# A gated two-way scan layer: its projections by Strassen's scheme with partial sums read from the banks, streamed by sixteen rows

## The chip, the core and the metric

The kernel runs on one NeuronCore of a Trainium2 chip, in float32. The metric is the device time of one execution in microseconds. The engines are PE (TensorE, matrix products), DVE (VectorE), ACT (ScalarE), POOL (GpSimd) and SP (SyncE, which issues all DMAs here); each runs its own queue in order, and they meet at semaphores. PE writes only to PSUM, eight banks of 128 partitions by 512 float32 values.

## What is computed

Four layers run one after another over four images of 512 channels by 64 by 64. Layer 0 is an attention layer, layer 1 a residual block of mixed-expert convolutions, layer 2 a linear attention. The change is in layer 3:

```python
C = input.shape[1]                                    # 512
x = jnp.einsum('bchw,oc->bohw', input, w_proj) + b_proj[None, :, None, None]
x_gate = x[:, :C]
x_scan = x[:, C:]
X_cum = _ds_cumsum(x_scan, discount, axis=2)          # y_t = d*y_{t-1} + x_t down the rows
X_cum = _ds_cumsum(X_cum, discount, axis=3)           # and along each row
gated = x_gate * jax.nn.sigmoid(X_cum)
return input + gamma * gated
```

The kernel runs the two sums in the other order, along the rows first, which gives the same.

So each image needs two products of a 512 by 512 weight with the 512 by 4096 image, one for the scan and one for the gate, two discounted running sums per channel, a sigmoid, a multiplication and the residual.

## The kernel before

An image lies in SBUF as four tiles `xs[pr]`, one per *pair* `pr` of column blocks: 128 partitions by four channel blocks (`kc`, or `m` for outputs) by 1024 columns, which are sixteen image rows. The images run one after another through `layer0` to `layer3`; while layer 3 of one image runs, tiles of the next are loaded as their buffers come free. PE's instructions keep the order in which the program writes them. The order on the other engines is set once, when the program is built: a planner takes, at its own reckoning of times, what is ready, earlier in the program first. Buffers come from pools with a fixed number each; where none is free, an instruction waits for the last reader of one. Two pools of PSUM matter: `pair_psum`, three tiles of two banks each, and `bank`, two tiles of one bank. Of SBUF pools, `bigp` has three tiles of 17 KB per partition, `xpool` five of 16 KB, `fourp` six of 4 KB, `blkp` seven of 2 KB, and `wlate` one of 16 KB.

Layer 2 ends with `add_values(pr, ms)` (lines 607 to 615, the products in L612, the addition in L615): for each channel block `m` two half-height products into a pair tile `wv`, which DVE adds to `xs`. Layer 3 then works by output channel block `m`. `scanned(m)` goes over the four pairs: eight products into a pair tile `ps` (L636), an ACT eviction with the bias into `s` (L638, tile `rows`), a DVE scan along the rows (L639), and an ACT copy that turns sixteen rows into columns of a second large tile `t` (L643, tile `cols`). When all 64 rows are there, four DVE scans run down the columns (L647), each followed by a sigmoid on ACT, written back in row order (L649). The scans take their discount from a tile `disc` whose entry at the start of each row or column is zero, so that one instruction of 1024 elements serves sixteen rows or columns. `gated(m, s)` makes eight products per pair into `pg` (L659), and DVE multiplies them with the sigmoids (L661) and adds the residual (L662); SP stores the result. The order is scanned 0, scanned 1, gated 0, scanned 2, gated 1, scanned 3, gated 2, gated 3; the additions of layer 2's values for pairs 1 to 3 stand between the products of scanned 0. The profile counts each float32 product of the program as two matmul instructions.

The weights `wproj` are loaded into `wlate` when layer 1's transformed values leave it (L76, issued after the last `conv2` in layer 2). `wc` (L358 to 361) is one `bigp` tile with layer 1's mixed weights and, behind them, `qs`, layer 2's query features.

Of the kernel before, what the change touches and what calls it, by code (L numbers as in the profile page):

```python
# [8 lines left out]
F32 = mybir.dt.float32  # L9
AF = mybir.ActivationFunctionType  # L10
ALU = mybir.AluOpType
# [3 lines left out]
B, C, H, W = 4, 512, 64, 64  # L15
P = 128
HW = H * W
NB = 512
NBLK = HW // NB
ROWS = NB // W  # L20
KC = C // P
D = 64
NT = HW // P
TPB = NB // P
NPAIR = NBLK // 2
E = 8
NPIECE = KC + 9 + KC
# [6 lines left out]
BQK, BPROJ, DISC, RB, SCALE, GAM2, GAM3 = 24, 25, 33, 37, 45, 46, 47  # L34
BQ2, BK2 = 48, 49
NPRM = 50
RING = 12


SUM_LO, SUM_HI = 1e-26, 1e30  # L40
# [3 lines left out]
def unshifted(ctx: ExitStack, tc: tile.TileContext, fits, x, wqkv_t, wout_t, router_t,  # L44
# [3 lines left out]
    nc = tc.nc  # L48
    const = ctx.enter_context(tc.tile_pool(name="const", bufs=1))
    wlate = ctx.enter_context(tc.tile_pool(name="wlate", bufs=1))  # L50
    xpool = ctx.enter_context(tc.tile_pool(name="xpool", bufs=5))
    bigp = ctx.enter_context(tc.tile_pool(name="bigp", bufs=3))
# [5 lines left out]
    def pair_psum(name):  # L58
        return ps.tile([P, 2, NB], F32, tag="s", name=name, bufs=3)

    def bank(name, shape=(P, NB)):
        return ps.tile(list(shape), F32, tag="acc", name=name)

    def four(name):
        return fourp.tile([P, 2, NB], F32, tag="four", name=name)

    def block(name, shape=(P, NB)):
        return blkp.tile(list(shape), F32, tag="blk", name=name)

    def flat(t):  # L70
        return t.rearrange("p h n -> p (h n)")

    def late_weights(src, shape, name):

        t = wlate.tile(shape, F32, tag="late", name=name)
        nc.sync.dma_start(t, src)  # L76
        return t

    def load_x(b):

        tiles = []
        for pr in range(NPAIR):
            t = xpool.tile([P, KC, 2 * NB], F32, tag="x", name=f"x_{b}_{pr}")
            nc.sync.dma_start(t, x[b, :, pr * 2 * NB:(pr + 1) * 2 * NB].rearrange("(kc p) n -> p kc n", p=P))
            tiles.append(t)
        return tiles


    wqkv_sb = const.tile([P, KC, 3 * D], F32, tag="wqkv", name="wqkv_sb")
    nc.sync.dma_start(wqkv_sb, wqkv_t.rearrange("(kc p) o -> p kc o", p=P))  # L90
    xs = load_x(0)
    prm_sb = const.tile([P, NPRM], F32, tag="prm", name="prm_sb")
    nc.sync.dma_start(prm_sb, prm)
    def col(i, n=1):
        return prm_sb[:, i:i + n]
# [17 lines left out]
    ones = const.tile([P, P], F32, tag="ones", name="ones")  # L113
# [241 lines left out]

    def layer1(b, xs, rw, mix):

        wcq = bigp.tile([P, NPIECE + 4 * NPAIR, P], F32, tag="big", name=f"wc_{b}")  # L358
        wc = wcq[:, 0:NPIECE, :]
        qs = wcq[:, NPIECE:, :].rearrange("p (a j) c -> p a (j c)", a=NPAIR)  # L360
        nc.scalar.copy(wc[:, 0:KC, :], mix)
        def mix_experts(j, n, pool, tag):
            ex = pool.tile([P, 4, E, P], F32, tag=tag, name=f"ex_{b}_{j}")
# [31 lines left out]
        for pr in range(NPAIR):  # L395
            y = pair_psum(f"c1_{b}_{pr}")
# [69 lines left out]
                nc.vector.scalar_tensor_tensor(xm, flat(y), bn_s[:, 2 + m:3 + m], xm, ALU.mult, ALU.add)  # L466
                nc.scalar.activation(xm, xm, AF.Relu, bias=bn_t[:, 2 + m:3 + m])

        return conv2, conv3, qs

    def layer2(b, xs, conv2, conv3, qs):

        ks = small.tile([P, NPAIR], F32, tag="ks", name=f"ks_{b}")
        g = bank(f"g_{b}", (P, C))
# [77 lines left out]
        h2[2] = conv2(2)  # L552
        conv3(1, h2[1])
        h2[3] = conv2(3)
        wproj_sb = late_weights(wproj_t.rearrange("(kc p) o -> p kc o", p=P), [P, KC, 2 * C], f"wproj_{b}")
        features(1, (0, 1))()
        conv3(2, h2[2])
        rest = features(0, (0, 1))
# [48 lines left out]
        def add_values(pr, ms=range(KC)):  # L607
            for m in ms:
# [4 lines left out]
                                     start=True, stop=True)  # L613
                xm = xs[pr][:, m, :]
                nc.vector.tensor_tensor(xm, flat(y), xm, ALU.add)  # L615
        return normed, add_values, wproj_sb

    def layer3(b, xs, normed, add_values, wproj_sb):


        def scanned(m):
            s = bigp.tile([P, HW], F32, tag="big", name=f"rows_{b}_{m}")
            t = bigp.tile([P, W, H], F32, tag="big", name=f"cols_{b}_{m}")
            disc = flat(four(f"disc_{b}_{m}"))
            nc.scalar.activation(disc, ones[:, 0:1].to_broadcast([P, 2 * NB]), AF.Copy, scale=col(DISC + m))
            nc.gpsimd.memset(disc.rearrange("p (r w) -> p r w", w=W)[:, :, 0:1], 0.0)
            for pr in range(NPAIR):
                if m == 0 and pr == 0:
                    add_values(0)
                blk = slice(pr * 2 * NB, (pr + 1) * 2 * NB)  # L630
                y = pair_psum(f"ps_{b}_{m}_{pr}")
                for h in range(2):
                    if m == 0 and pr + 1 < NPAIR:
                        add_values(pr + 1, (2 * h, 2 * h + 1))
                    for kc in range(KC):
                        nc.tensor.matmul(y[:, h, :], wproj_sb[:, kc, C + m * P:C + (m + 1) * P],  # L636
                                         xs[pr][:, kc, h * NB:(h + 1) * NB], start=kc == 0, stop=kc == KC - 1)
                nc.scalar.activation(s[:, blk], flat(y), AF.Identity, bias=col(BPROJ + KC + m))  # L638
                nc.vector.tensor_tensor_scan(s[:, blk], disc, s[:, blk], 0.0, ALU.mult, ALU.add)  # L639

                rows = s[:, blk].rearrange("p (h w) -> p w h", w=W)
                r0 = pr * 2 * ROWS
                nc.scalar.copy(t[:, :, r0:r0 + 2 * ROWS], rows)  # L643
            tf = t.rearrange("p w h -> p (w h)")
            for c in range(NPAIR):
                blk = slice(c * 2 * NB, (c + 1) * 2 * NB)
                nc.vector.tensor_tensor_scan(tf[:, blk], disc, tf[:, blk], 0.0, ALU.mult, ALU.add)  # L647
                c0 = c * 2 * ROWS
                nc.scalar.activation(s.rearrange("p (h w) -> p w h", w=W)[:, c0:c0 + 2 * ROWS, :],  # L649
                                     t[:, c0:c0 + 2 * ROWS, :], AF.Sigmoid)  # L650
            return s

        def gated(m, s):
            for pr in range(NPAIR):
                blk = slice(pr * 2 * NB, (pr + 1) * 2 * NB)
                y = pair_psum(f"pg_{b}_{m}_{pr}")
                for h in range(2):
                    for kc in range(KC):
                        nc.tensor.matmul(y[:, h, :], wproj_sb[:, kc, m * P:(m + 1) * P],  # L659
                                         xs[pr][:, kc, h * NB:(h + 1) * NB], start=kc == 0, stop=kc == KC - 1)  # L660
                nc.vector.scalar_tensor_tensor(s[:, blk], flat(y), col(BPROJ + m), s[:, blk], ALU.add, ALU.mult)  # L661
                nc.vector.scalar_tensor_tensor(s[:, blk], s[:, blk], col(GAM3), xs[pr][:, m, :],  # L662
                                               ALU.mult, ALU.add)
                nc.sync.dma_start(out[b, m * P:(m + 1) * P, blk], s[:, blk])

        sf = scanned(0)
        for m in range(KC):
            nxt = scanned(m + 1) if m + 1 < KC else None
            gated(m, sf)
            sf = nxt  # L670

    with tc.manual_schedule(engines={mybir.EngineType.PE}):
        for b in range(B):
            convs = layer1(b, xs, *layer0(b, xs))
            nxt = load_x(b + 1) if b + 1 < B else None
            tail = layer2(b, xs, *convs)
            layer3(b, xs, *tail)
            xs = nxt


    ends = small.tile([P, 2], F32, tag="ends", name="ends", bufs=1)
# [449 lines left out]
```

## Time and profile before

| | |
|---|---|
| median of the runs | 2866.96 us (2866.65 to 2868.54, three runs) |
| the profiled execution's own time | 2869.1 us |
| its span | 2867.2 us |
| PE busy in it | 2785.5 us, 97% |
| DVE busy | 1817.0 us, 63% |
| ACT busy | 1182.1 us, 41% |
| mean granted clock of PE | 0.991 |

The profile is of one execution; spans and times are in microseconds unless marked ns. Its groups of instructions give a line of the kernel, engine, operation, output and input by the program's names, shapes and count, then busy time, mean duration of one, and the idle time of the engine just ahead of them with what ended it. PEld are weight loads, which run beside products. Matmuls are pipelined, so the time from one start to the next is shorter than the duration of one. The chain that ended last is followed back from the last instruction to what released it each time.

### The profile page before, as it was taken

How to read it: one execution, taken by the hardware profiler on the slowest of the kernel's cores; microseconds unless marked ns; L12 is line 12 of the kernel's file. 1: busy time of each engine (PE TensorE's matmuls, PEld its weight loads, DVE VectorE, ACT ScalarE, POOL GpSimd, SP SyncE). 2: the span in 40 equal slices, each digit the busy share in tenths (PEclk: the TensorE clock that was granted, in tenths of full speed). 3: DMA queues.
4: the chain of work that ended last, by engine and by line, in shares of the span. 5: the costliest groups of instructions: out<-in, count | busy, mean ns of one | idle time of the engine just before them, and what ended most of it. 6: DMA issues, size and time to landing. Idle time of an engine off the chain costs nothing.

```text
span 2867.2 us, 24918 instructions
## 1 busy us (share of the span) xinstructions
PE 2785.5 (97%) x10174; PEld 1178.8 (41%) x10174; DVE 1817.0 (63%) x1827; ACT 1182.1 (41%) x1131; POOL 11.4 (0%) x34
## 2 busy tenths in 40 slices
PE   8999989999999999999999998999999999899998
PEld 3333444444333344444433334544443333454443
DVE  2687866564378786555437879566544786956644
ACT  4545243443454414353344442535334544143531
POOL 1000000000000000000000000000000000000000
PEclk9999999999999999999999999999999999999999
DMA  4000210011300021001220002100131000100001
GB/s 178 1 1 0 96 59 1 0 52 59 125 1 1 1 95 59 1 0 59 86 90 1 1 1 95 59 1 6 53 118 58 1 1 28 68 30 1 22 37 60
DMA packets 31485, 115.12 MB, mean 40 GB/s; under 512 B 2432, under 2 KB 3456, under 8 KB 31360
## 3 DMA queue, kind: packets, MB, share of 16 engines
q1 hardware_dynamic: 31360, 113.43, 10.4%
q8 instruction: 82, 1.34, 0.2%
q14 instruction: 43, 0.35, 0.0%
HBM read 79.86 MB, written 33.55 MB: 40 GB/s over the span
## 4 chain that ended last, share of the span: by engine, by line
PE 85%; DVE 11%; ACT 2%; issue 1%; DMA 0%; SPq 0%; ACTq 0%; DVEq 0%
PE s L213 16%; PE av L228 16%; PE ps L636 16%; PE pg L659 15%; PE z L485 4%; PE kq L174 4%; PE c L464 3%; DVE wc L368 2%; PE wv L612 2%; PE vv L174 2%; PE xtr L527 2%; PE g L544 2%; PE c L444 1%; PE y L267 1%; DVE nrm L573 1%; DVE t L412 1%
## 5 line engine op out<-in xcount | busy, mean ns | idle before, releaser
L213 PE MATMUL s<-qv,key 64*128 64x512 f32 x2048 | 468.8, 602 | 1.8 <-ACT ring L216 1.8
L636 PE MATMUL ps<-x,wproj 128*128 128x512 f32 x1024 | 447.2, 595 | 0.0
L221 DVE TENSOR_TENSOR acc<-acc,ring 128x1024 f32<-128x1024 f32 x312 | 381.7, 1224 | 100.0 <-ACT ring L216 71.3
L659 PE MATMUL pg<-x,wproj 128*128 128x512 f32 x1024 | 441.4, 592 | 0.0
L216 ACT ACTIVATE ring<-s 128x1024 f32<-128x1024 f32 x336 | 317.6, 1038 | 223.8 <-PE s L213 223.5
L639 DVE TENSOR_TENSOR_SCAN rows<-disc,rows 128x1024 f32<-128x1024 f32 x64 | 146.7, 2292 | 259.4 <-ACT rows L638 237.4
L228 PE MATMUL av<-ring,qv 128*64 128x512 f32 x1344 | 304.5, 595 | 0.0
L213 PEld LDWEIGHTS s<-qv,key 64*128 64x128 f32 x2048 | 189.0, 187 | 274.9 <-issue 172.9
L636 PEld LDWEIGHTS ps<-x,wproj 128*128 128x128 f32 x1024 | 192.8, 190 | 251.7 <-issue 242.3
L659 PEld LDWEIGHTS pg<-x,wproj 128*128 128x128 f32 x1024 | 194.7, 190 | 244.7 <-issue 242.8
L221 DVE TENSOR_TENSOR acc<-acc,ringx 128x1024 f32<-128x1024 f32 x168 | 205.5, 1223 | 102.4 <-ACT ringx L216 90.1
L216 ACT ACTIVATE ringx<-s 128x1024 f32<-128x1024 f32 x176 | 172.1, 1040 | 207.0 <-PE s L213 207.0
L638 ACT ACTIVATE rows<-ps,prm_sb 128x1024 f32<-128x1024 f32 x64 | 71.0, 1110 | 290.6 <-PE ps L636 290.6
L643 ACT COPY cols<-rows 128x1024 f32<-128x1024 f32 x64 | 125.6, 1963 | 151.9 <-DVE rows L639 151.9
L228 PEld LDWEIGHTS av<-ring,qv 128*64 128x64 f32 x1344 | 93.4, 137 | 198.5 <-issue 198.5
L228 PE MATMUL av<-ringx,qv 128*64 128x512 f32 x704 | 167.2, 598 | 0.0
L647 DVE TENSOR_TENSOR_SCAN cols<-disc,cols 128x1024 f32<-128x1024 f32 x64 | 141.4, 2272 | 32.4 <-ACT cols L643 32.4
L464 PE MATMUL c<-h,wc 128*128 128x512 f32 x256 | 125.3, 644 | 33.6 <-ACT h L456 33.6
L661 DVE SCALAR_TENSOR_TENSOR rows<-pg,prm_sb,rows 128x1024 f32<-128x1024 f32 x64 | 81.8, 1278 | 116.6 <-PE pg L659 116.6
L649 ACT ACTIVATE rows<-cols 128x1024 f32<-128x1024 f32 x64 | 128.1, 2002 | 41.3 <-DVE cols L647 41.3
L174 PE MATMUL kq<-x,wqkv_sb 128*64 128x512 f32 x512 | 115.8, 606 | 9.5 <-DMA x<-in_x_dram 9.0
L466 DVE SCALAR_TENSOR_TENSOR x<-c,bn_s,x 128x1024 f32<-128x1024 f32 x64 | 81.3, 1281 | 56.3 <-PE c L464 56.3
(162 smaller groups left out, 2529.5 us busy)
## 6 DMA issues: line engine op xcount, KB each, us to landing
x<-in_x_dram SPq DMA_DIRECT2D x16, 2048.0 KB, 8.6
out_dram<-rows SPq DMA_DIRECT2D x64, 512.0 KB, 2.6
ex<-in_experts_dram SPq DMA_DIRECT2D x12, 1536.0 KB, 9.5
ex<-in_experts_dram SPq DMA_DIRECT2D x8, 2048.0 KB, 9.5
wproj<-in_wproj_t_dram SPq DMA_DIRECT2D x4, 2048.0 KB, 10.1
wv_sb<-in_wv_t_dram SPq DMA_DIRECT2D x1, 1024.0 KB, 9.6
wqkv_sb<-in_wqkv_t_dram SPq DMA_DIRECT2D x1, 384.0 KB, 3.3
wout_sb<-in_wout_t_dram SPq DMA_DIRECT2D x2, 128.0 KB, 13.9
```

Of the source, the lines that this page charges most:

```text
L174: nc.tensor.matmul(y[h * D:(h + 1) * D, :], wqkv_sb[:, kc, col0:col0 + D], xs[pr][:, kc, h * NB:(h + 1) * NB], start=kc == 0, stop=kc == K ...
L213: nc.tensor.matmul(s[:, h, :], key[r, kt * P:(kt + 1) * P], qry[r, pr * NB:(pr + 1) * NB], start=True, stop=True)
L216: nc.scalar.activation(p, s, AF.Exp)
L221: nc.vector.tensor_tensor(accs[pr], accs[pr], p, ALU.add)
L228: nc.tensor.matmul(avs[pr][h * D:(h + 1) * D, :], vt[:, kt, :], ring[i % RING][:, h, :], start=kt == 0, stop=kt == NT - 1)
L464: nc.tensor.matmul(y[:, h, :], wc[:, KC + 9 + m, :], h2[:, h, :], start=True, stop=True)
L636: nc.tensor.matmul(y[:, h, :], wproj_sb[:, kc, C + m * P:C + (m + 1) * P], xs[pr][:, kc, h * NB:(h + 1) * NB], start=kc == 0, stop=kc == K ...
L639: nc.vector.tensor_tensor_scan(s[:, blk], disc, s[:, blk], 0.0, ALU.mult, ALU.add)
L643: nc.scalar.copy(t[:, :, r0:r0 + 2 * ROWS], rows)
L647: nc.vector.tensor_tensor_scan(tf[:, blk], disc, tf[:, blk], 0.0, ALU.mult, ALU.add)
L649: nc.scalar.activation(s.rearrange("p (h w) -> p w h", w=W)[:, c0:c0 + 2 * ROWS, :], t[:, c0:c0 + 2 * ROWS, :], AF.Sigmoid)
L659: nc.tensor.matmul(y[:, h, :], wproj_sb[:, kc, m * P:(m + 1) * P], xs[pr][:, kc, h * NB:(h + 1) * NB], start=kc == 0, stop=kc == KC - 1)
```

## The change

The product of weights and image is cut two by two: weights by output half and input half, the image by input half (channel blocks 0, 1 and 2, 3) and by the two blocks of 512 columns in a pair. Seven products of 256 by 256 by 512 take the place of eight, in Winograd's form of Strassen's scheme. A *tile* `(pr, j)` yields, for one pair, the output blocks `j` and `j + 2`; a `Sums` block makes it for the scan and a `Gates` block for the gate. An image has eight tiles. Iteration `i` of a loop of nine runs the Sums of tile `i` and the Gates of tile `i - 1`, product by product in turn; the first and the last iteration have one block alone.

Each block has one bank `x`, in which products 1, 6, 7 and 4 are added up one after another, and a pair `zy`, with product 2 in one bank and 5 and 3 in the other. After products 1, 6 and 7 ACT evicts the running sum of `x` with the bias into `e[0..2]`, each before the next product is added to that bank. DVE forms the four outputs from `zy`, `x` and `e`. The four sums of weights S1 to S4 are formed on DVE when the quarters of the weights have come, by eight loads in place of one; the sums of image parts T1 to T4 are formed per pair by four DVE subtractions and additions, after its values have been added.

The scans no longer wait for all 64 rows: each tile scans its sixteen rows along, turns them by ACT, adds the carried state of the row above (`carry`, times the discount) to the first entry of each column, scans down sixteen rows, keeps the last entry as the next carry, and takes the sigmoid. Scans are half as long (512), with one discount tile `along` for the rows and one `down`, reset when `j` changes, for the columns. `add_values` steps of the next pair stand ahead of product 2 of a block. The loads of the next image's tiles are issued inside the loop, every second iteration.

```diff
-        wcq = bigp.tile([P, NPIECE + 4 * NPAIR, P], F32, tag="big", name=f"wc_{b}")
+        wcq = bigp.tile([P, NPIECE + 1 + 4 * NPAIR, P], F32, tag="big", name=f"wc_{b}")
         wc = wcq[:, 0:NPIECE, :]
-        qs = wcq[:, NPIECE:, :].rearrange("p (a j) c -> p a (j c)", a=NPAIR)
+        qs = wcq[:, NPIECE + 1:, :].rearrange("p (a j) c -> p a (j c)", a=NPAIR)
         nc.scalar.copy(wc[:, 0:KC, :], mix)
...
-        wproj_sb = late_weights(wproj_t.rearrange("(kc p) o -> p kc o", p=P), [P, KC, 2 * C], f"wproj_{b}")
+        weights = load_quarters(b)
...
+    def load_quarters(b):
+        wq = wlate.tile([P, 4, 2, 2, 2 * P], F32, tag="late", name=f"wq_{b}")
+        sx = xpool.tile([P, 4, 2, 2, 2 * P], F32, tag="x", name=f"sx_{b}")
+        wr = wproj_t.rearrange("(k c p) (s m o) -> k c m p s o", c=2, p=P, s=2, m=2)
+        for q, (m, k) in enumerate(((0, 0), (0, 1), (1, 1), (1, 0))):
+            for c in range(2):
+                nc.sync.dma_start(wq[:, q, c], wr[k, c, m])
+        a11, a12, a22, a21 = (wq[:, q] for q in range(4))
+        s2, s3, s4 = (sx[:, q] for q in range(3))
+        fl = lambda t: t.rearrange("p c s o -> p (c s o)")
+        nc.vector.tensor_tensor(fl(s3), fl(a11), fl(a21), ALU.subtract)
+        nc.vector.tensor_tensor(fl(a21), fl(a21), fl(a22), ALU.add)
+        nc.vector.tensor_tensor(fl(s2), fl(a21), fl(a11), ALU.subtract)
+        nc.vector.tensor_tensor(fl(s4), fl(a12), fl(s2), ALU.subtract)
+        spare = fl(sx[:, 3]).rearrange("p (i n) -> p i n", i=2)
+        nc.gpsimd.memset(fl(sx[:, 3]).rearrange("p (w r) -> p w r", r=R2)[:, :, 0], 0.0)
+        return {1: a11, 2: a12, 3: s4, 4: a22, 5: a21, 6: s2, 7: s3}, spare
+    def layer3(b, xs, add_values, weights, wcq):
+        weights, down = weights
+        carry = wcq[:, KC * TPB:KC * TPB + 2, :].rearrange("p i (m w) -> p (i m) w", w=W)
+        others, rowsums, cols = {}, {}, {}
+        along = wcq[:, 0:KC * TPB, :].rearrange("p (m j) c -> p m (j c)", m=KC)
+        nc.gpsimd.memset(along.rearrange("p m (r w) -> p (m r) w", w=W)[:, :, 0], 0.0)
+        for m in range(KC):
+            nc.scalar.activation(along[:, m, :].rearrange("p (r w) -> p r w", w=W)[:, :, 1:],
+                                 ones[:, 0:1, None].to_broadcast([P, ROWS, W - 1]), AF.Copy, scale=col(DISC + m))
+        def set_down(j):
+            for i in range(2):
+                nc.scalar.activation(down[:, i, :].rearrange("p (w r) -> p w r", r=R2)[:, :, 1:],
+                                     ones[:, 0:1, None].to_broadcast([P, W // 2, R2 - 1]), AF.Copy,
+                                     scale=col(DISC + j + 2 * i))
+            cols["set"] = j
+        def sum_x(pr):
+            t = bigp.tile([P, 4, 2, NB], F32, tag="big", name=f"t_{b}_{pr}")
+            xv = xs[pr].rearrange("p k (h n) -> p k h n", h=2)
+            b11, b12, b21, b22 = xv[:, 0:2, 0], xv[:, 0:2, 1], xv[:, 2:4, 0], xv[:, 2:4, 1]
+            t1, t2, t3, t4 = (t[:, i] for i in range(4))
+            nc.vector.tensor_tensor(t3, b22, b12, ALU.subtract)
+            nc.vector.tensor_tensor(t2, t3, b11, ALU.add)
+            nc.vector.tensor_tensor(t1, b12, b11, ALU.subtract)
+            nc.vector.tensor_tensor(t4, b21, t2, ALU.subtract)
+            others[pr] = {1: b11, 2: b21, 3: b22, 4: t4, 5: t1, 6: t2, 7: t3}
+        class Block:
+            def __init__(self, kind, pr, j):
+                self.kind, self.pr, self.j = kind, pr, j
+                name = f"{b}_{kind}_{pr}_{j}"
+                self.name = name
+                self.x = bank(f"sx_{name}")
+                self.zy, self.done = None, set()
+                self.bias = [col(BPROJ + kind * KC + m) for m in (j, j + 2)]
+                self.e = [block(f"e{i}_{name}") for i in range(3)]
+            def product(self, k):
+                if k == 2:
+                    self.zy = pair_psum(f"zy_{self.name}")
+                y = self.x if k in (1, 6, 7, 4) else self.zy[:, 0 if k == 2 else 1, :]
+                w, v = weights[k], others[self.pr][k]
+                for c in range(2):
+                    nc.tensor.matmul(y, w[:, c, self.kind, self.j * P:(self.j + 1) * P], v[:, c, :],
+                                     start=c == 0 and k in (1, 2, 5), stop=c == 1,
+                                     skip_group_check=k not in (1, 2, 5))
+                self.done.add(k)
+                if k in (1, 6, 7):
+                    i = (1, 6, 7).index(k)
+                    nc.scalar.activation(self.e[i], y, AF.Identity, bias=self.bias[i // 2])
+                if k in (5, 7) and {5, 7} <= self.done:
+                    self.fifth()
+                elif k == 4:
+                    self.fourth()
+        class Sums(Block):
+            def fifth(self):
+                self.s = [flat(four(f"s{i}_{self.name}")) for i in range(2)]
+                nc.vector.tensor_tensor(self.s[1][:, NB:], self.zy[:, 1, :], self.e[2], ALU.add)
+            def fourth(self):
+                nc.scalar.activation(self.s[1][:, :NB], self.x, AF.Identity, bias=self.bias[1])
+            def end(self):
                 for h in range(2):
...
+                    nc.vector.tensor_tensor(self.s[0][:, h * NB:(h + 1) * NB], self.zy[:, h, :], self.e[h], ALU.add)
+                if cols.get("set") != self.j:
+                    set_down(self.j)
+                for i in (1, 0):
+                    m, s = self.j + 2 * i, self.s[i]
+                    for h in range(2):
+                        sh = s[:, h * NB:(h + 1) * NB]
+                        nc.vector.tensor_tensor_scan(sh, along[:, m, :], sh, 0.0, ALU.mult, ALU.add)
+                    sr = s.rearrange("p (r w) -> p w r", w=W)
+                    tf = flat(four(f"t{i}_{self.name}"))
+                    t = tf.rearrange("p (w r) -> p w r", w=W)
+                    nc.scalar.copy(t, sr)
+                    if self.pr > 0:
+                        nc.vector.scalar_tensor_tensor(t[:, :, 0], carry[:, m, :], col(DISC + m), t[:, :, 0],
+                                                       ALU.mult, ALU.add)
+                    for h in range(2):
+                        th = tf[:, h * NB:(h + 1) * NB]
+                        nc.vector.tensor_tensor_scan(th, down[:, i, :], th, 0.0, ALU.mult, ALU.add)
+                    if self.pr < NPAIR - 1:
+                        nc.scalar.copy(carry[:, m, :], t[:, :, R2 - 1])
+                    nc.scalar.activation(sr, t, AF.Sigmoid)
+                rowsums[self.pr, self.j] = self.s
+        class Gates(Block):
+            def fifth(self):
+                self.s = rowsums.pop((self.pr, self.j))
+                nc.vector.tensor_tensor(self.e[2], self.zy[:, 1, :], self.e[2], ALU.add)
+            def fourth(self):
+                s = self.s[1][:, :NB]
+                nc.vector.scalar_tensor_tensor(s, self.x, self.bias[1], s, ALU.add, ALU.mult)
+                s = self.s[1][:, NB:]
+                nc.vector.tensor_tensor(s, s, self.e[2], ALU.mult)
+                self.add_x(1)
+            def end(self):
                 for h in range(2):
...
+                    e, s = self.e[h], self.s[0][:, h * NB:(h + 1) * NB]
+                    nc.vector.tensor_tensor(e, self.zy[:, h, :], e, ALU.add)
+                    nc.vector.tensor_tensor(s, s, e, ALU.mult)
+                self.add_x(0)
+            def add_x(self, i):
+                m, s = self.j + 2 * i, self.s[i]
+                nc.vector.scalar_tensor_tensor(s, s, col(GAM3), xs[self.pr][:, m, :], ALU.mult, ALU.add)
+                nc.sync.dma_start(out[b, m * P:(m + 1) * P, self.pr * 2 * NB:(self.pr + 1) * 2 * NB], s)
+        tiles = [(pr, (pr + j) % 2) for pr in range(NPAIR) for j in range(2)]
+        between = {0: [(1, 0), (1, 1)], 1: [(1, 2), (1, 3)], 2: [(2, 0), (2, 1)], 3: [(2, 2), (2, 3)],
+                   4: [(3, 0), (3, 1)], 5: [(3, 2), (3, 3)]}
+        nxt = []
+        add_values(0)
+        sum_x(0)
+        for i in range(len(tiles) + 1):
+            blocks = [Sums(1, *tiles[i])] if i < len(tiles) else []
+            blocks += [Gates(0, *tiles[i - 1])] if i else []
+            todo = list(between.get(i, ()))
+            for n, k in enumerate((1, 2, 6, 7, 5, 4, 3) if len(blocks) > 1 else (1, 2, 6, 5, 7, 4, 3)):
+                for s in blocks:
+                    if n in (1, 3) and todo:
+                        pr, m = todo.pop(0)
+                        add_values(pr, (m,))
+                        if m == KC - 1:
+                            sum_x(pr)
+                    s.product(k)
+            for s in blocks:
+                s.end()
+            if i and i % 2 == 0 and b + 1 < B:
+                nxt.append(load_pair(b + 1, i // 2 - 1))
+        return nxt
...
             convs = layer1(b, xs, *layer0(b, xs))
-            nxt = load_x(b + 1) if b + 1 < B else None
-            tail = layer2(b, xs, *convs)
-            layer3(b, xs, *tail)
-            xs = nxt
+            xs = layer3(b, xs, *layer2(b, xs, *convs))
```

Of the lines with a minus sign the diff above leaves out the bodies of `scanned` and `gated`, which are told in the section on the kernel before.

More of the change, by code (lines that the diff above doesn't have):

```diff
@@ L37 @@
 RING = 12
+R2 = 2 * ROWS
 SUM_LO, SUM_HI = 1e-26, 1e30
@@ L77, in late_weights, with load_pair @@
         return t
[L79 to L86, printed above, removed]
+    def load_pair(b, pr):
+        t = xpool.tile([P, KC, 2 * NB], F32, tag="x", name=f"x_{b}_{pr}")
+        nc.sync.dma_start(t, x[b, :, pr * 2 * NB:(pr + 1) * 2 * NB].rearrange("(kc p) n -> p kc n", p=P))
+        return t
     wqkv_sb = const.tile([P, KC, 3 * D], F32, tag="wqkv", name="wqkv_sb")
     nc.sync.dma_start(wqkv_sb, wqkv_t.rearrange("(kc p) o -> p kc o", p=P))
-    xs = load_x(0)
+    xs = [load_pair(0, pr) for pr in range(NPAIR)]
     prm_sb = const.tile([P, NPRM], F32, tag="prm", name="prm_sb")
@@ L467, in conv3, with layer2 @@
                 nc.scalar.activation(xm, xm, AF.Relu, bias=bn_t[:, 2 + m:3 + m])
-        return conv2, conv3, qs
-    def layer2(b, xs, conv2, conv3, qs):
+        return conv2, conv3, wcq, qs
+    def layer2(b, xs, conv2, conv3, wcq, qs):
         ks = small.tile([P, NPAIR], F32, tag="ks", name=f"ks_{b}")
@@ L615, in add_values @@
                 nc.vector.tensor_tensor(xm, flat(y), xm, ALU.add)
[L616 to L631, printed above, removed]
-                for h in range(2):
[L633 to L656, printed above, removed]
-                for h in range(2):
[L658 to L670, printed above, removed]
@@ new lines, in layer2 @@
+        return add_values, weights, wcq
+    def load_quarters(b):
[15 more added lines that the diff above has]
+        return {1: a11, 2: a12, 3: s4, 4: a22, 5: a21, 6: s2, 7: s3}, spare
```

## The prediction, made before the change was run

> **What bounds the kernel now.** I read the page's busy shares first, then the chain that ended last, then the groups and the windows of layer 3, and last the order of time where layer 3 starts.
>
> ```profile
> PE 2785.5 (97%) x10174; PEld 1178.8 (41%) x10174; DVE 1817.0 (63%) x1827; ACT 1182.1 (41%) x1131; POOL 11.4 (0%) x34
> PE 85%; DVE 11%; ACT 2%; issue 1%; DMA 0%; SPq 0%; ACTq 0%; DVEq 0%
> PE s L213 16%; PE av L228 16%; PE ps L636 16%; PE pg L659 15%; PE z L485 4%; PE kq L174 4%; PE c L464 3%; DVE wc L368 2%; PE wv L612 2%; PE vv L174 2%; PE xtr L527 2%; PE g L544 2%; PE c L444 1%; PE y L267 1%; DVE nrm L573 1%; DVE t L412 1%
> ```
>
> PE is busy 97% of the span, and layer 3's two products (ps, pg) are 31% of the chain: fewer matmuls there shorten the end, as long as nothing takes PE's place.
>
> ```profile
> L636 PE MATMUL ps<-x,wproj 128*128 128x512 f32 x1024 | 447.2, 595 | 0.0
> L659 PE MATMUL pg<-x,wproj 128*128 128x512 f32 x1024 | 441.4, 592 | 0.0
> L639 DVE TENSOR_TENSOR_SCAN rows<-disc,rows 128x1024 f32<-128x1024 f32 x64 | 146.7, 2292 | 259.4 <-ACT rows L638 237.4 <-issue 22.0
> L647 DVE TENSOR_TENSOR_SCAN cols<-disc,cols 128x1024 f32<-128x1024 f32 x64 | 141.4, 2272 | 32.4 <-ACT cols L643 32.4
> L643 ACT COPY cols<-rows 128x1024 f32<-128x1024 f32 x64 | 125.6, 1963 | 151.9 <-DVE rows L639 151.9
> L649 ACT ACTIVATE rows<-cols 128x1024 f32<-128x1024 f32 x64 | 128.1, 2002 | 41.3 <-DVE cols L647 41.3
> L662 DVE SCALAR_TENSOR_TENSOR rows<-rows,prm_sb,x 128x1024 f32<-128x1024 f32 x64 | 82.3, 1285 | 2.3
> L615 DVE TENSOR_TENSOR x<-wv,x 128x1024 f32<-128x1024 f32 x64 | 74.4, 1216 | 22.3 <-PE wv L612 22.3
> L447 DVE TENSOR_TENSOR dq<-c,sp 128x512 f32<-128x512 f32 x16 | 11.0, 689 | 35.7 <-ACT sp L446 35.7
> L446 ACT COPY sp<-c 128x512 f32<-128x512 f32 x16 | 9.4, 585 | 70.7 <-PE c L444 70.7
> ```
>
> The columns are busy us, mean ns of one, idle before. The two matmul groups have no idle at all; those on DVE and ACT wait for PE or for each other.
>
> ```profile
> 1236.00:1438.60 202.60, 202.60 (x474) 89.52 (x475) 106.64 (x62) 79.44 (x51) 0.00 (x0) 1.00 0.16 60
> ```
>
> This is layer 3 of the second image: length, then busy PE, PEld, DVE, ACT. PE is full, DVE has 96 us to spare, ACT 123. Next come PE's chain and timeline rows.
>
> ```profile
> 1273.78 27.47 PE pg L659 x64
> ...
> 1080.76 9.73 PE L464 MATMUL c<-h,wc 128*128 128x512 f32 x16 [8.41 <-ACT h L456]
> ...
> 1098.10 7.03 PE L464 MATMUL c<-h,wc 128*128 128x512 f32 x16
> ...
> 1208.00 3.70 PE L636 MATMUL ps<-x,wproj 128*128 128x512 f32 x8
> 1211.63 1.99 PE L612 MATMUL wv<-wc,kv 64*128 64x512 f32 x8
> ```
>
> 64 matmuls in 27.47 us is 0.429 each, the price used below (the 592 ns is latency). Eight wv are 1.95 us, so one add_values step (four) is 0.98; 1211.63 − 1208.00 − 8 × 0.429 leaves 0.2 us for the switch to them.
>
> **Matmuls, on the path.** An image now issues 1024 / 4 × 2 = 512 (each counted product is two instructions). The change issues 8 tiles × 2 kinds × 7 products × 2 halves of the sum × 2 instructions = 448. 64 × 0.429 = 27.5 us an image, 109.9 in four. A product is 4 × 0.429 = 1.72 us, a full iteration (seven for Sums S, seven for Gates G) 24.0, with two add_values steps ("mixed", iterations 1 to 5) 26.0, plus 2 × 0.2.
>
> **DVE, beside it.** From 1.22 us for 1024 elements and 0.69 for 512 the fixed part is 0.16, so a half scan is (2.28 + 0.16) / 2 = 1.22; its bounds are 1.14 (half the row) and 2.29. A tile's Sums: 3 × 0.69 + 8 × 1.22 + two column fixes of 64 elements (between the 0.15 and 0.28 us of the smallest rows; 0.2, in six of eight tiles) = 12.1. Its Gates: 7 × 0.69 + 2 × 1.28 = 7.4. Together 19.5; a mixed iteration adds 2 × 1.22 for the value sums and, every other time, 4 × 1.22 for T1 to T4: 24.4 on average, against PE's 26.4. Over the image that is 196 of some 208 us, where 129 of 236 are used now (106.6 in the window above, 22 before it). DVE fits, with next to no slack, so order decides.
>
> **ACT** per tile: four copies and sigmoids 8.0, seven evictions 0.6 each, two carry copies and the discount rows about 1.2: 13.4 of 24. It fits too.
>
> **The new wait.** A mixed iteration wants four pair buffers (step, S's, step, G's) from three. G's product 2 needs the first step's buffer, so its addition on DVE. From PE's end of a tile (t = 0) unhindered PE wants that buffer at t = 7.1. DVE, taking early whatever is ready early: S's product 4 ends at −5.15, evicted by −4.3; first-half scan of the upper rows to −3.1; G's fourth step (0.69 + 0.69 + 1.28) to −0.4; S's last addition to 0.3; column scans with fix to 3.0; one row scan to 4.2; G's end (same three sizes) to 6.8. ACT meanwhile runs sigmoid 3.0 to 5.0, copy to 7.0. If the addition, ready at 4.6, goes next, it ends at 8.0 and PE waits 1.0 us; if the column scans behind the copy go first, 3.8. The trace cannot show this order, fixed at build; a step put early would wait 0. I take the middle of the two, 2.4, × 5 = 12.0 us an image. All of PE's later products queue behind G's product 2.
>
> **Small terms per image.** Three evictions per block must read the bank x between products that add to it. Nearest rows: ACT starts some 0.2 after PE, 0.59 for the read. Bare, 16 blocks × 3 × 0.8 = 38 us, more than the gain; but the other block's 1.72 us product lies between. What shows is the single-block iterations 0 and 8, where product 4 follows 7: 0.9 each, 1.8. In iterations 6 and 7 a read of G behind a 2.0 us sigmoid: 0.4 each, 0.8. Six more switches to wv than now: 1.2. Weight sums, 4 × 1.22 = 4.9 on DVE in layer 2: 0 if in the idle 11.8 us that DVE has near 1163, 4.9 if ahead of key transposes; 1.5. Sum with the wait: 17.3 us.
>
> The Trainium skill, "PSUM — Partial Sum Buffer", section on bank collisions, says that two engines must never touch one bank at once, even at other addresses; that speaks against reading running sums. By it alone, with no interleaving, the 38 us above would stand.
>
> **Edits at nothing.** The eight weight loads bring the same 2 MB as wproj (10.1 us to landing) in 1 KB runs; four times the first small-run load (384 KB in 3.3) gives 13.2. They are issued near 1113 and needed 90 us later; uncovered, 10 to 13 an image. The x loads go out tile by tile on SP behind the stores; the last is issued just as layer 0 starts and its pair is multiplied 32 us later (kq 1438.6 to 1470.9), against 8.6 to land. Discount rows: ACT and POOL, under 3 us, in ACT's idle time. T1 to T4 of pair 0 lie beside two products. The tail, one half-size step more: 1 us once.
>
> **Sum.** −109.9 + 4 × 17.3 + 1 = −39.7 us. The profiled execution has span 2867.2 and time 2869.1, so 2827.5 and 2829.4; applied to the median of 2866.96, which is 2.1 below the profiled time, 2827.
>
> **Rivals.**
> *Whole gain*: DVE's planned order puts the value additions early, so that PE never waits; 1.8 + 1.2 = 3.0 an image stay: −109.9 + 12 + 1 = −97, 2770. For it: DVE's 24.4 is below 26.4. Against it: its work comes in one run of 11 us at each tile's end, just when PE wants buffers.
> *Slower*: DVE's queue becomes the bound. Its place is the tile's end: each column scan waits at the queue's head for its 2.0 us copy, with ready additions behind it. A mixed iteration is then 24.4 + 2 × 2.0 = 28.4 against 26.4, so 2.0 + 3.8 = 5.8 × 5 = 29.0, with 1.8 + 0.8 + 1.2 + 4.9: 37.7 an image, −109.9 + 150.8 + 1 = +42, 2909. It decides from 27.2 us of waits an image, 4.4 per mixed iteration with the 5.3 of small terms. For it: L647's idle is all waits for that copy, once per four scans now, twice per tile then. Against it: other ready work is there to fill the 2 us.
> *Clock*: after the 8.41 us wait above, 16 matmuls took 9.73 instead of 7.03, 2.7 lost; after the 1.3 us wait ahead of the first wv (24 in 5.85) nothing. My waits lie nearer the second, so nothing is taken.
>
> The Trainium skill, "TensorE: Matmul & The Clock Gate", section on the HAM clock gate, halves the clock after an idle window of about 3.4 us; if each 3.8 us wait did that, up to 1.7 us estimated each, 34 us in all, would come on top. The rows here show only the 8.41 us case.
>
> That fewer matmuls are not issued is excluded by the loops.
>
> **How the numbers follow.** The forecast, 2800 (waits of 1.0) to 2870 (waits of 3.8, weight sums uncovered), has 0.47, of which 0.06 falls within 0.2% (5.7 us, about what a measurement can tell from no change). Whole gain: 0.23. Slower: 0.30, as DVE's slack is 2 us in 26 and I cannot see its order. Faster is 0.41 + 0.23 = 0.64, same 0.06, slower 0.30. The range, 2767 to 2900, takes in the whole gain and most of the slower case.
>
> **What would show it.** Right: about 1792 layer 3 matmuls at 0.429; DVE near 87% busy (195 of 225 us) between layer 3's start and end; layer 3 near 225 us an image instead of 236; PE waiting before products for value additions (x). Whole gain: PE without gaps there. Wrong: DVE full and PE's gaps of 4 us or more in each mixed iteration, or gaps on ACT's evictions, which I count at almost nothing; or layer 2 longer by over 5 us an image.

## The result, and the profile after

The changed kernel takes 3004.81 us (3002.67 to 3007.02) against 2867.19 for the kernel before: 1.0479 times as long (95% interval 1.0461 to 1.0497), 138 us more, beyond the range of 2767 to 2900. These are lines of the page of the changed kernel: the span, the busy time of each engine with its instructions, and the costliest groups in question (busy time and mean ns of one, then the idle time before them).

```profile
span 3003.7 us, 25338 instructions
...
PE 2760.3 (92%) x9918; PEld 1145.7 (38%) x9918; DVE 2044.3 (68%) x2339; ACT 1277.6 (43%) x1379; POOL 10.8 (0%) x26
...
L693 ACT ACTIVATE e<-sx,prm_sb 128x512 f32<-128x512 f32 x192 | 130.0, 684 | 334.8 <-PE sx L687 334.8
...
L719 DVE TENSOR_TENSOR_SCAN s<-wc,s 128x512 f32<-128x512 f32 x128 | 154.9, 1216 | 27.7 <-ACT s L706 26.4
...
L729 DVE TENSOR_TENSOR_SCAN t<-sx,t 128x512 f32<-128x512 f32 x128 | 148.9, 1205 | 14.3 <-ACT t L723 14.3
```

The waits of PE in the changed kernel, longest in total first (us in total, times, longest):

```profile
PE zy L687 <- DVE x L614: 85.8, 20, 6.1
PE sx L687 <- ACT e L693: 57.6, 24, 3.9
PE c L463 <- ACT h L455: 33.6, 4, 8.4
```

PE issues 256 matmuls fewer (9918 against 10174), 109.9 us by 0.429 each, yet it is busy for only 25.2 us less, and it is idle for 243.4 us where it was for 81.7. So the span's +136.5 is −25.2 + 161.7. Two waits stand out, neither of which the kernel before had: 20 times, once in each mixed iteration, PE waits for the value addition (x, L614), 0.6 us in iteration 1 and 3.5 to 6.1 in iterations 2 to 5; and 24 times for an eviction (e, L693). The third row is old. Most of the missing part of the 109.9 lies in the clock (65.5 of 84.7 us, by the hand-ordered kernel below), as PE's own order of time shows in the second image (start, length, what, and the wait ahead of it):

```profile
1302.16 3.25 PE L687 MATMUL zy<-x,wq 128*128 128x512 f32 x4 [3.53 <-DVE x L614]
1305.21 7.50 PE L687 MATMUL sx<-t,sx 128*128 128x512 f32 x16
1312.55 3.60 PE L687 MATMUL zy<-t,wq 128*128 128x512 f32 x8
...
1337.19 3.51 PE L687 MATMUL zy<-x,wq 128*128 128x512 f32 x4 [6.10 <-DVE x L614]
1340.53 7.03 PE L687 MATMUL sx<-t,sx 128*128 128x512 f32 x16
...
1440.45 6.49 PE L687 MATMUL sx<-t,sx 128*128 128x512 f32 x8 [3.88 <-ACT e L693]
```

Four matmuls take 1.98 in this view at full clock, eight 3.60, sixteen 7.03. Behind the waits four take 3.25 (and the sixteen after them 7.50) or 3.51, and eight take 6.49: 1.7, 1.5 and 2.9 us are lost behind these three. Layer 3 of this image as a window (length, then busy PE, PEld, DVE, ACT, the granted clock):

```profile
1238.90:1503.50 264.60, 226.62 (x507) 93.36 (x508) 178.32 (x197) 110.67 (x117) 0.00 (x0) 0.92 0.14 52
```

The granted clock is 0.92 where it was 1.00, and DVE is busy 67% of the time: not full. Why PE waits is in DVE's order. The start of iteration 3, which PE begins at 1322.85, in DVE's order of time in the same kernel:

```profile
1321.54 1.28 DVE L756 SCALAR_TENSOR_TENSOR s<-s,prm_sb,x 128x1024 f32<-128x1024 f32 x1
1322.74 1.28 DVE L710 TENSOR_TENSOR s<-zy,e 128x512 f32<-128x512 f32 x2
...
1324.17 1.21 DVE L719 TENSOR_TENSOR_SCAN s<-wc,s 128x512 f32<-128x512 f32 x1
1325.31 2.31 DVE L729 TENSOR_TENSOR_SCAN t<-sx,t 128x512 f32<-128x512 f32 x2
1327.54 1.19 DVE L719 TENSOR_TENSOR_SCAN s<-wc,s 128x512 f32<-128x512 f32 x1
...
1332.49 2.33 DVE L729 TENSOR_TENSOR_SCAN t<-sx,t 128x512 f32<-128x512 f32 x2
...
1335.91 2.35 DVE L614 TENSOR_TENSOR x<-wv,x 128x1024 f32<-128x1024 f32 x2
```

And two rows of ACT's order of time there, the sigmoid of the first output block and the turn of the second into columns:

```profile
1327.90 1.98 ACT L732 ACTIVATE s<-t 128x1024 f32<-128x1024 f32 x1
1329.69 1.92 ACT L723 COPY t<-s 128x1024 f32<-128x1024 f32 x1
```

The last row scan starts at 1327.54, behind the first column scans, and on ACT the sigmoid of the first block stands ahead of the second turn into columns. That turn starts 6.8 us into the iteration; the second column scans and a step of the gates wait behind it on DVE, and the value additions come at 13.1 us, at the end of the whole run of work. PE had asked for the buffer 8.2 us in, 6.10 before its wait ended at 1337.19. Earlier, from 1304.4 to 1314.5, DVE had been idle for 10.08 us.

### The profile page after: what moved, and what is told of

Same layout as the page of the kernel before. It is cut to its first block, busy times and chain, and to the rows that moved or that the text cites. A ratio compares the mean times of both kernels' runs of the same rounds, so it can differ in the third digit from the quotient of the medians.

```text
span 3003.7 us, 25338 instructions
## 1 busy us (share of the span) xinstructions
PE 2760.3 (92%) x9918; PEld 1145.7 (38%) x9918; DVE 2044.3 (68%) x2339; ACT 1277.6 (43%) x1379; POOL 10.8 (0%) x26
## 5 line engine op out<-in xcount | busy, mean ns | idle before, releaser
L687 PE MATMUL sx<-t,sx 128*128 128x512 f32 x512 | 267.5, 674 | 51.2 <-ACT e L693 46.7
L693 ACT ACTIVATE e<-sx,prm_sb 128x512 f32<-128x512 f32 x192 | 130.0, 684 | 334.8 <-PE sx L687 334.8
L687 PE MATMUL zy<-x,wq 128*128 128x512 f32 x256 | 147.4, 711 | 85.8 <-DVE x L614 85.8
L687 PEld LDWEIGHTS sx<-t,sx 128*128 128x128 f32 x512 | 111.0, 221 | 207.9 <-issue 144.6
L719 DVE TENSOR_TENSOR_SCAN s<-wc,s 128x512 f32<-128x512 f32 x128 | 154.9, 1216 | 27.7 <-ACT s L706 26.4
L729 DVE TENSOR_TENSOR_SCAN t<-sx,t 128x512 f32<-128x512 f32 x128 | 148.9, 1205 | 14.3 <-ACT t L723 14.3
L723 ACT COPY t<-s 128x1024 f32<-128x1024 f32 x64 | 126.2, 1972 | 41.3 <-DVE s L719 41.3
L732 ACT ACTIVATE s<-t 128x1024 f32<-128x1024 f32 x64 | 126.8, 1981 | 23.1 <-DVE t L729 23.0
L687 PE MATMUL sx<-t,wq 128*128 128x512 f32 x256 | 118.1, 602 | 10.9 <-ACT e L693 10.9
L484 PE MATMUL z<-x,wqk_sb 128*64 128x512 f32 x512 | 119.8, 623 | 8.3 <-DVE x L465 8.3
```

What stands on the lines that cost most here:

```text
L484: nc.tensor.matmul(z[h * D:(h + 1) * D, i, :], wqk_sb[:, kc, w * D:(w + 1) * D], xs[pr][:, kc, h * NB:(h + 1) * NB], start=kc == 0, stop=k ...
L687: nc.tensor.matmul(y, w[:, c, self.kind, self.j * P:(self.j + 1) * P], v[:, c, :], start=c == 0 and k in (1, 2, 5), stop=c == 1, skip_grou ...
L693: nc.scalar.activation(self.e[i], y, AF.Identity, bias=self.bias[i // 2])
L719: nc.vector.tensor_tensor_scan(sh, along[:, m, :], sh, 0.0, ALU.mult, ALU.add)
L723: nc.scalar.copy(t, sr)
L729: nc.vector.tensor_tensor_scan(th, down[:, i, :], th, 0.0, ALU.mult, ALU.add)
```

## The experiments

Two theories: the *order* of DVE's and ACT's queues makes PE wait, and each wait costs clock besides; or DVE and ACT have *too much to do*. A third, that reading running sums from a bank is what costs, goes with them.

**The chain at the tile's end left out.**

```diff
-                    (turn into columns, carry, column scans, carry kept)
-                    nc.scalar.activation(sr, t, AF.Sigmoid)
+                    nc.scalar.activation(s, s, AF.Sigmoid)
```

> The changed kernel without the sums down the columns: copy into columns, carry, column scans are left out, the sigmoid is taken in row order. 2.7 us of DVE and 2.3 us of ACT per output block go, and with them the chain at the tile's end. Theory A: PE's waits in layer 3 fall to under 5 us an image; the gain of 110 us shows, less some 13 us of layer 2 and the single-block iterations: 2770 to 2820. Rival C: waits on evictions stay, 2880 or more. Rival B would also give under 2850.

Measured: 2806.2 us, ratio 0.9781 (0.9765 to 0.9797). PE waits 8.2 us in all for evictions and 5.4 for value additions. Reading running sums is thus not what costs: all 192 such reads are still there. The second theory foresaw a time under 2850 here as well, so work and order are not told apart by this.

**Streaming alone**, with eight plain products per output block and pair, sums evicted from pair tiles:

```diff
+            products(y, pr, KC + m)                  # eight matmuls, as before
+            nc.scalar.activation(s, flat(y), AF.Identity, bias=col(BPROJ + KC + m))
             (row scans, turn, carry, column scans, sigmoid of 16 rows as in the change)
```

> One part alone: layer 3 streams by sixteen rows with the carried column state and the half-length scans, but with the plain eight products per output block and pair, evicted from pair tiles as in the kernel before; two blocks of sums run ahead of the gates. Theory A: per 14.7 us of PE DVE has 9 and no running sum is read, so PE never waits for long: 2860 to 2890, the time of before. Rival B: the scan chain by sixteen rows itself holds PE up: 2920 or more.

Measured: 2873.33 us, ratio 1.0019 (1.0009 to 1.0029). The carried state and the half-length scans cost 5.5 us where no partial sum is read between products and every pair tile is free in time; in layer 3 of the second image PE has no wait of its own.

**The value steps moved** from before product 2 to before product 5:

```diff
-                    if n in (1, 3) and todo:
+                    if n in ((4, 5) if i else (1, 3)) and todo:
```

> The two value steps of an iteration stand before product 5 instead of before product 2, in iterations 1 to 5; nothing else differs from the changed kernel (3004.8 us). Theory A (queue order: PE's waits come from value additions that stand behind the tile's end on DVE, and evictions that stand behind a sigmoid on ACT, and each wait of over 2 us costs about 1.7 us of halved clock besides): the 85.8 us of waits ahead of product 2 and some 30 us of clock go, part of it comes back at evictions; 2890 to 2950. Rival B (DVE and ACT have simply too much to do per tile): the wait moves to another place, within 15 us of 3005. Rival C (reading running sums from a bank is what costs): within 15 us of 3005, with the waits on evictions grown.

Measured: 3014.9 us, ratio 1.0504 (1.0486 to 1.0522). My theory's number failed, and both rivals' was met: the 85.8 us at value additions went, but the waits on evictions grew from 57.6 to 147.0 us (60 times). ACT's order of time there in iteration 3, which PE begins at 1330.04:

```profile
1336.91 1.93 ACT L723 COPY t<-s 128x1024 f32<-128x1024 f32 x1
1338.74 0.68 ACT L693 ACTIVATE e<-sx,prm_sb 128x512 f32<-128x512 f32 x1
...
1342.14 0.30 ACT L731 COPY wc<-t 128x64 f32<-128x64 f32 x1 [2.14 <-DVE t L729]
1342.35 1.94 ACT L732 ACTIVATE s<-t 128x1024 f32<-128x1024 f32 x1
...
1344.66 1.25 ACT L693 ACTIVATE e<-sx,prm_sb 128x512 f32<-128x512 f32 x2
```

and PE's, behind that eviction:

```profile
1345.38 6.15 PE L687 MATMUL sx<-t,sx 128*128 128x512 f32 x8 [3.93 <-ACT e L693]
```

ACT sits 2.14 us waiting for the column scans to keep the carry, takes the sigmoid, and only then makes the eviction that PE's next product waits for. Each wait that goes uncovers the next one in the same late chain. By itself that fits the theory of too much work as well; the third theory fits too, and falls by the kernel without the chain above.

**Filling the wait**, to see what the clock costs: two more of the same product ahead of the Gates block's product 2.

```diff
+                    if k == 2 and i and i in between and s is blocks[1]:
+                        for c in (0, 1, 0, 1):
+                            nc.tensor.matmul(f.zy[:, 0, :], ..., start=c == 0, stop=c == 1)   # f = blocks[0]
```

> In iterations 1 to 5, product 2 of the Sums block is issued three times over instead of once (each time from zero, same result) just ahead of the Gates block's product 2, where PE waits 3.5 to 6.1 us: 20 times 3.4 us more of matmuls, 69 us. Theory A: the waits there shrink by about what is added, and the halved clock behind them does not come: 15 to 30 us faster than the changed kernel, 2975 to 2990. If the slow matmuls behind a wait have nothing to do with the wait: 3005 to 3025.

Measured: 2966.96 us, ratio 1.0346 (1.0329 to 1.0363): 38 us *less* than the changed kernel, with 69 us of matmuls more (160 × 0.429). PE is busy 2785.7 us against 2760.3, only 25 more, so 43 us of slow clock are gone, more than the 15 to 30 us that I had expected the whole to give. The waits for value additions fall from 85.8 to 26.0 us (12 left, up to 2.5). PE in the second image:

```profile
1285.02 1.13 PE L611 MATMUL wv<-wc,kv 64*128 64x512 f32 x4
1286.08 3.70 PE L780 MATMUL zy<-x,wq 128*128 128x512 f32 x8
1289.69 1.98 PE L687 MATMUL zy<-x,wq 128*128 128x512 f32 x4
```

Where the filler (L780) covers the wait, the product behind it runs at full speed, 1.98 for four.

**The order written by hand.** The same instructions, with the value steps before product 5 and four of them in iteration 0. The text of the loop is laid out anew, and in one kernel the planner keeps its freedom, in three others one queue or both are held to the text (shortened here, without its conditions):

```diff
+            s.product(1)
+            ps_.downward(1)          # column scans, carry kept, sigmoid of block j + 2
+            g.product(1)             # its eviction stands between the two sigmoids on ACT
+            ps_.downward(0)          # those of block j, ahead of the gates' end
+            pg.add_x(1); pg.end()
...
-            xs = layer3(b, xs, *layer2(b, xs, *convs))
+            with tc.manual_schedule(engines={DVE, Activation}):
+                xs = layer3(b, xs, *l2)
```

Both queues by hand:

> The same instructions as the changed kernel; in layer 3 DVE and ACT issue in an order written by hand: evictions of running sums and the turns into columns ahead of the sigmoids that would hold them up, column scans before the gates' end, value steps before product 5 (when DVE is idle) with four in iteration 0, the sums T one iteration ahead. Theory A (queue order): waits on evictions and value additions fall to under 1 us each and the clock stays up: 2775 to 2830. Rival B (too much work per tile for DVE and ACT): 2900 or more whatever the order.

Neither:

> The same program text as the hand-ordered one, but the planner again sets the order on DVE and ACT, by its own reckoning of when each is ready. Theory A: the planner's reckoning, not the place in the text, makes the order, so evictions again stand behind sigmoids: 2900 to 3010, at least 50 us more than the hand-ordered one. If the place in the text was the fault: within 20 us of the hand-ordered one.

ACT alone:

> As the hand-ordered kernel (2813.9 us), but only ACT's order in layer 3 is written by hand; DVE's is the planner's. It tells which queue held PE up once the value steps stand before product 5 (planner for both: 2904.9). If ACT's queue alone did it: within 15 us of 2814. If DVE's order decides as well: 2840 to 2890.

DVE alone:

> As the hand-ordered kernel (2813.9), but only DVE's order in layer 3 is by hand, ACT's is the planner's (ACT alone by hand: 2893.6; planner for both: 2904.9). If both queues must follow one order: 2850 to 2905. If DVE's queue is what decides: within 15 us of 2814.

| order held to the text on | us | ratio to before (95%) |
|---|---|---|
| neither | 2904.9 | 1.0126 (1.0109 to 1.0143) |
| ACT | 2893.57 | 1.0085 (1.0070 to 1.0100) |
| DVE | 2819.11 | 0.9823 (0.9807 to 0.9839) |
| both | 2813.93 | 0.9812 (0.9795 to 0.9828) |

With both by hand the loss of 138 us is a gain of 54 with the same matmuls, scans and evictions: the theory of too much work falls, that of the order stands. The four kernels have the same text, and only the queues held to it differ. DVE's queue decides, alone within 6 us of both; ACT's alone brings 11 us, and 2893.57 lies a little above the slower of the two ranges put down for it. The waits on evictions did not all fall under 1 us, as I had expected with both by hand: 22.0 us are left in 17 waits, up to 2.1. The layout of the text alone, with the planner's order, gives 100 us of the 191; how much of this is the place of the value steps is not shown. DVE in the hand-ordered kernel, at the start of iteration 2 (PE begins it at 1239.82):

```profile
1239.03 1.23 DVE L708 TENSOR_TENSOR_SCAN s<-wc,s 128x512 f32<-128x512 f32 x1
1240.17 4.55 DVE L725 TENSOR_TENSOR_SCAN t<-sx,t 128x512 f32<-128x512 f32 x4
```

ACT there, the second turn into columns and the last sigmoid:

```profile
1240.35 2.00 ACT L714 COPY t<-s 128x1024 f32<-128x1024 f32 x1 [1.49 <-DVE s L708]
...
1245.56 2.03 ACT L728 ACTIVATE s<-t 128x1024 f32<-128x1024 f32 x1
```

and PE, products 6 and 7 of both blocks:

```profile
1246.69 7.03 PE L687 MATMUL sx<-t,sx 128*128 128x512 f32 x16
```

Of block j one row scan alone is left for the tile's end; the other is done long before, as this row of the next tile shows (PE ends that tile at 1266.37):

```profile
1258.12 1.22 DVE L708 TENSOR_TENSOR_SCAN s<-wc,s 128x512 f32<-128x512 f32 x1
```

The second turn into columns starts 0.5 us into the iteration (in iteration 3 as well) instead of 6.8, all four column scans follow in one run, the last sigmoid starts at 5.7, and PE's sixteen matmuls of products 6 and 7 run in 7.03 with no wait. This window is layer 3 of the same image there:

```profile
1189.45:1412.00 222.55, 217.27 (x528) 90.49 (x530) 183.89 (x203) 114.22 (x120) 0.00 (x0) 0.99 0.18 67
```

222.6 us, of which the last 3.2 are layer 0's, with DVE busy 83% and the clock at 0.99.

**The value steps before product 2 again**, with the hand order fitted to that:

```diff
+            pg.free()                # the gates' last reads of their pair tile
+            step()                   # first value step, its addition on DVE
+            s.product(2)
+            ps_.downward(0)
```

> Hand order on DVE and ACT, but the value steps of iterations 1 to 4 stand ahead of product 2 again, as in the change; on DVE the gates' last reads of their pair tile and the first value addition stand ahead of the second column scans. My prediction's working says that G's product 2 need not wait if the addition comes that early (0 to 1.0 us): then 2805 to 2830. If the fourth buffer itself is missing there, whatever the order: 4 waits of 3.5 us or more an image with their clock, 2860 to 2910.

Measured: 2811.69 us, ratio 0.9801 (0.9785 to 0.9817). The place that I had blamed is harmless if the addition stands early on DVE: three pair tiles are enough. The kernel does a little more than the text says: in iteration 0 it issues product 2 of the Sums block twice, 16 matmuls in all (9934 against 9918), by 0.429 each some 6.9 us of its time.

**Layer 2's weight sums, and the evictions of iterations 1 and 8.** The first kernel is the hand-ordered one with the four sums of weights written behind the products of pair 1; the second also sets the gates' first eviction ahead of the sigmoid in two iterations.

```diff
         products(1, ahead(2))
+        sum_weights()
...
+            if i in (1, len(tiles)):
+                g.product(1)
             if ps_:
                 ps_.downward(1)
```

> The hand-ordered kernel with the four weight sums of layer 2 written after the products of pair 1 instead of ahead of layer 2's features, where PE waits 1.8 us for the DVE additions behind them. If the weight sums are what lengthens layer 2 by some 3 us an image: 6 to 13 us less than the hand-ordered one, 2801 to 2808. If they were hidden: within 3 us of 2814.

> The kernel with later weight sums, and in iterations 1 and 8 the gates' first eviction stands ahead of the sigmoid on ACT, where PE now waits 1.8 and 2.1 us: 4 waits of 2 us and some halved clock go in part; 2 to 12 us below the run with later weight sums.

Measured: 2802.3 us, ratio 0.977 (0.9757 to 0.9784), and 2800.58 us, ratio 0.9771 with the same interval. The weight sums were worth 11.6 us by the medians, 2.9 an image. The second edit made no difference that these runs can tell: its five runs lie between 2799.78 and 2809.79, those of the first between 2800.94 and 2802.66. Both beat the kernel before by 2.3%.

## Why the prediction was wrong

*Right.* The matmuls: 256 fewer, 0.429 us each at full clock. The durations: a half scan was put at 1.22 and took 1.216 and 1.205. The single estimates that missed were small: evictions 0.68 instead of 0.59, column fixes 0.31 to 0.33 instead of 0.2. DVE's added busy time was 227 us where 284 had been reckoned ((195 − 129 + 4.9) × 4): the durations of its instructions add up to 268 more, and those in a run overlap, 4.55 us for four scans of 1.2. DVE had room, as the sum said. The bound put on the weight loads was short, as four times 384 KB are 1.5 MB and not 2, but each load landed in 4.7 us and no wait of PE names them; DVE waits 33.1 us in all for them ahead of the weight sums.

*The step that failed* is the one headed "The new wait": "DVE, taking early whatever is ready early". The place was right: the buffer for G's product 2, and the addition behind the tile's end. But the working left one of S's last additions and one row scan to the tile's end, and the planned order left two of each there; the hand-ordered kernel does the earlier ones behind product 5, the scan 8 us ahead of the tile's end. So the first column scans ended 4.8 us into iteration 3 instead of 3.0, and the second turn, behind the sigmoid on ACT, at 8.8 instead of 7.0. Then the second column scans went first, the worse of the two cases, but two steps of the gates' end (L751, L756), which the working had done by 6.8, stood among them ahead of the addition. The first addition ended at 14.3, not at 8.0 or 10.9. The wait was 85.8 / 20 = 4.3 us a mixed iteration instead of 2.4.

*Evictions* had been counted at 0.8 + 1.8 = 2.6 us an image; they cost 57.6 / 4 = 14.4 before their clock, of which iterations 6 and 7 have 7.4 (0.8 in the sum), iteration 8 has 3.8 and iteration 1 has 2.3. The working let the other block's product cover each read, which holds only if ACT is free; ACT stood in its own order waiting for the same late column scans.

*The clock* had been put at nothing. Two rows were at hand, 8.4 us with a loss of 2.7 and 1.3 us with none, and "My waits lie nearer the second" chose between two ends with nothing measured in between. Against the hand-ordered kernel, which issues the same matmuls, PE's busy time is 2760.3 − 2694.8 = 65.5 us longer and its idle time 127.6 longer; together the 193.1 between the two spans. So a third of the distance between the two is clock. The prediction's estimate from the Trainium skill, "TensorE: Matmul & The Clock Gate", HAM clock gate, by which the clock halves after an idle window of about 3.4 us, was up to 34 us. It was nearer than nothing, and still short: here waits of 2.24 us cost clock too (four matmuls behind one took 3.52 us).

*The rivals.* "Slower" had the sign and the place, with additions behind the column scans, but at +42 only; without clock and with evictions at 2.6 it could not reach +138. Its premise, that DVE's queue becomes the bound, did not come: DVE is busy 67% of layer 3 and idle for 10 us at a stretch. Of the signs named for being wrong, gaps of 4 us or more before product 2 came in three of five mixed iterations, and gaps on evictions came; a full DVE did not. "Whole gain" had 2770; the order by hand with later weight sums reaches 2802. The weight sums, 1.5 us an image in the sum, were worth 2.9.

The Trainium skill's rule in "PSUM — Partial Sum Buffer", bank collisions, that two engines must never touch one bank at once, had been weighed against the change. It did not decide: PE waits for each of these reads where it is late, and with the reads all in place and the chain left out it waits 8.2 us for evictions in the whole kernel.

What stays open: why the planner's times make this order was not traced, nor which place in DVE's order matters most. Shown is that the order, and not the work, costs the time.

## What to carry to other kernels

When a dense engine is fed by others, and one of these is nearly full by the sum (here 24.4 of 26.4 us), the sum says that the work fits but not that it flows: write the queues down in the order in which the program's planner will set them, and ask where the last link of the chain stands. A change that adds cross-engine steps to every tile is worth trying a second time with those queues ordered by hand before it is given up. Price each expected PE wait of 2 us or more with the clock that may follow it.

## What the runs showed of the hardware

The clock falls for waits far shorter than I had thought, and between 2.0 and 2.5 us the length alone does not decide. Take the groups of four and of eight matmuls in layer 3, over all the traces here. None of the 51 that follow a wait of 1.2 to 1.95 us is slow; of the 52 behind waits of 1.98 to 2.55 us, 28 are, by 0.4 to 1.7 us; all 57 behind waits of 3.48 us or more are, by 1.2 to 2.9 us. One and the same place of the hand-ordered kernel, in iteration 8, has waits of 2.01, 2.09, 2.01 and 2.01 us in the four images, and the four matmuls behind them take 1.98, 3.18, 2.74 and 1.98 us. Here is the second of them, and a longer wait in the kernel with both of the last edits, behind which they run at full speed:

```profile
1397.25 3.18 PE L687 MATMUL sx<-t,sx 128*128 128x512 f32 x4 [2.09 <-ACT e L692]
...
1399.63 1.98 PE L689 MATMUL sx<-t,sx 128*128 128x512 f32 x4 [2.27 <-ACT e L694]
```

What decides there is not shown. Matmuls that compute nothing new, put into the longer waits of the changed kernel, made it 38 us faster.
